# Mixture-of-experts block: the second expert product with its weights standing, each choice's result in a row of its own, and the sum moved into layer 1

## The chip, the cores and the metric

One core of a Trainium2 chip. The metric is the time of one execution on the device, in microseconds; the kernel before takes 15654.79 (median of 3 runs, 15653.87 to 15655.51). All data are fp32.

The engines are named as in the profile: PE multiplies matrices (PEld is its loading of the standing operand), DVE and ACT work on rows and columns of the on-chip memory, POOL does some of the same and issues the indirect transfers (scatters), SP issues the plain transfers. Each works through its own list of instructions in order.

## The reference

Two layers on an image batch x of 32 x 128 channels x 56 x 56. Layer 0 is a depthwise 7x7 convolution, a layer norm over the channels and a mixture of eight experts. T = 100,352 tokens, each with C = 128 values; every token goes to its two best experts, as far as these have room (cap = 15,680 rows for each):

```
xf      = layernorm(dwconv7x7(x))                  # T x C
logits  = xf @ Wg + bg ; top 2, softmax of the two -> wts
order   = argsort(-wts[:, 0])                      # strongest first
slot    = expert * cap + position in the expert    # those beyond cap are dropped
buf[slot] = xf rows ;  eb = buf as E x cap x C
h       = gelu(eb @ W1 + b1) ;  y = h @ W2 + b2    # C -> 4C -> C
moe     = sum over a token's two choices of y[slot] * gate
x       = x + xf (turned back to channels first) + layer_scale * moe
```

Layer 1 is a Mamba block on the result: a 1x1 convolution cv1, a depthwise 3x3 branch, a layer norm and a selective scan over the 3136 positions of each image with 256 channels and 16 states, a last 1x1 convolution, and x added.

## The kernel before

It runs through four stages, and the tensors between them lie in device memory.

Convolution and norm. The convolution is done with banded matrices on two image rows at a time, so a tile of TT = 112 rows of data is two image rows, in an order that is the reverse of the image's (partition p of a tile is position 55 - p of its row). The rows xf go to `res_d` (T x 128) in this reversed order.

Routing (from L478). The choices are ranked, and each token's two slots and gates come out as `slots` and `gates`. Meanwhile SP fills all slots of `buf_d` (L482 to L486) from one tile: zeros and, in column C + 1, the row number T. A row of `buf_d` has RW = 130 columns: the token's 128 values, its gate, and the number of its row in the result.

Dispatch (L840 to L863). 56 turns; each loads 14 x 128 rows of `res_d` into `xgs[0]` (L853), copies them to `xgs[1]` on ACT (L854), adds gate and row number on DVE (L856, L857; the row numbers `backs` are the same for both choices), and issues 28 scatters of 128 rows to `buf_d` on POOL (L859). Six pairs of buffers. Layer 1's weights are prepared in the middle (`weights`).

Experts (L914 to L957). For each expert 31 groups of up to GT x 128 = 512 rows (30 full ones and one of 320). A group is loaded (L945), turned on PE (L951, to `ept`), copied to `xc` on ACT (L953); the products of a group come one group later, in `products`: for each quarter k of the 512 hidden values `ph` = w1 times xc, Gelu on ACT to `hh` (L890, L893); then for each tile of 128 rows `py` += hh (standing) times w2 (moving, 128 columns; L897), so the result comes out with rows on partitions; bias and gate on DVE (L903, L906); and one scatter of 128 rows for each tile on POOL that adds to `res_d` (L911). The adding scatters of one expert are declared independent of each other (`apart`), those of two experts are not.

Layer 1 (`layer1`). 224 groups of 448 positions, 16 states each. The order of all instructions is written out: `PLAN` and `UNITS` give every step a time in units of one state, all steps of all groups are sorted by it and issued in this order. The scan runs on DVE (L1373), its products on DVE and POOL (L1397), the sum over states on PE (L1286), exponentials on ACT (L1354). For each group `fetch` loads the image's columns `x1` and the rows `yg` of `res_d`; `moe_pe` adds them on PE: `x1` times the identity, and each tile of `yg` turned by a product with `perm`, which also undoes the reversed order; `moe_act` copies the sum to `x1`. The matmul tiles `mm_tile` of layer 1 rotate over two banks.

## Time and profile before

| | us |
|---|---|
| median of 3 runs | 15654.79 |
| the profiled execution | 15660.14 |
| its span, first to last instruction | 15658.4 |
| first dispatch scatter (L859) starts | 1772.5 |
| last dispatch scatter starts | 3765.1 |
| first transpose of the experts (L951) | 3770.5 |
| last scatter of the experts (L911) starts | 5688.3 |
| first db product of layer 1 (L1336) | 5738.0 |

Busy time over the whole span: PE 12820.1 us (82%), PEld 7165.1 (46%), DVE 11115.5 (71%), ACT 10499.2 (67%), POOL 13201.9 (84%). The mean granted PE clock is 0.918.

The profile is one execution, seen instruction by instruction. A row of the groups reads: line, engine, operation, what is written from what, how often; busy time in all and mean of one in ns; idle time of the engine just before them and what ended it. The shares over the whole span are a mean over stages that differ, so stages are read one by one. Ends of PE's instructions are modelled and may overlap the next one; starts are the better measure.

### The profile page before, as it was taken

What the parts mean: (1) busy time and instruction counts of PE and PEld (TensorE: products, weight loads), DVE (VectorE), ACT (ScalarE), POOL (GpSimd) and SP (SyncE); (2) the same over time, 40 slices, a digit from 0 to 9 for tenths busy, and PEclk for the clock granted to TensorE, in tenths of its full rate; (3) what the DMA queues carried; (4) which work ended last, traced back from release to release, by engine and by line L of the source; (5) the groups of instructions that cost most, each with busy time, mean ns of one, the idle gap of its engine ahead of it and who ended that gap; (6) DMA issues with size and microseconds to landing.
All of it is one profiled execution on the core that took longest, in us unless ns stands there. A gap on an engine that the chain in (4) does not pass through costs nothing. (4 is left out here: it accounts for less than half of the span.)

```text
span 15658.4 us, 247520 instructions
## 1 busy us (share of the span) xinstructions
PE 12820.1 (82%) x92981; PEld 7165.1 (46%) x92981; DVE 11115.5 (71%) x11366; ACT 10499.2 (67%) x21038; POOL 13201.9 (84%) x6330
## 2 busy tenths in 40 slices
PE   7997200003999989999999999999999999999998
PEld 7996100002777754444444444444444444444444
DVE  2655500000111149999999999999999999999999
ACT  4555300001444458888888888888888888888887
POOL 2443377777888879999999999999999999999999
PEclk9997555556999999999999999999999999999999
DMA  8785522223555545555555555555555555555555
GB/s 266 232 234 165 189 78 78 78 78 68 72 71 72 70 102 184 183 185 184 183 186 184 183 184 185 183 184 186 185 183 184 185 183 183 185 185 184 183 183 169
DMA packets 1325280, 2520.85 MB, mean 161 GB/s; under 512 B 139352, under 2 KB 777136, under 8 KB 1316400
## 3 DMA queue, kind: packets, MB, share of 16 engines
q1 hardware_dynamic: 1127600, 2310.57, 46.9%
q0 software_dynamic: 196480, 194.45, 7.2%
q8 instruction: 732, 11.99, 0.3%
q14 instruction: 468, 3.83, 0.1%
HBM read 2129.06 MB, written 375.43 MB: 160 GB/s over the span
## 5 line engine op out<-in xcount | busy, mean ns | idle before, releaser
L1336 POOL TENSOR_TENSOR db<-du,bb 128x1792 f32<-128x1792 f32 x1792 | 6578.8, 3683 | 0.1
L1354 ACT ACTIVATE da<-dt,aneg 128x449 f32<-128x449 f32 x7168 | 4539.9, 637 | 375.4 <-DVE r L1095 113.0
L1373 DVE TENSOR_TENSOR_SCAN da<-da,db 128x898 f32<-128x898 f32 x2240 | 4522.2, 2019 | 0.6 <-issue 0.5
L1286 PE MATMUL py<-prod,ident 64*64 64x448 f32 x28672 | 3225.1, 547 | 121.7 <-DVE prod L1397 114.0
L1397 POOL TENSOR_TENSOR prod<-hs,cb 128x896 f32<-128x896 f32 x1344 | 2604.2, 1938 | 231.3 <-issue 156.7
L1397 DVE TENSOR_TENSOR prod<-da,cb 128x896 f32<-128x896 f32 x2240 | 2439.5, 1089 | 134.6 <-DMA cb<-bc_d 18.2
L859 POOL DMA_INDIRECT buf_d<-xg,slot x1568 | 1515.8, 967 | 482.0 <-issue 456.7
L911 POOL DMA_INDIRECT res_d<-ys,xb x984 | 1592.1, 1618 | 331.6 <-issue 286.2
L1373 DVE TENSOR_TENSOR_SCAN hs<-da,db 128x898 f32<-128x898 f32 x896 | 1785.6, 2014 | 0.1
L951 PE MATMUL ept<-ident,xb 128*128 128x128 f32 (+1 forms) x984 | 189.0, 274 | 1917.3 <-DMA xb<-buf_d 1917.3
L1286 PEld LDWEIGHTS py<-prod,ident 64*64 64x64 f32 x28672 | 1008.5, 132 | 1559.8 <-issue 1065.4
L1126 PE MATMUL p_xm<-te,wk 128*128 128x448 f32 x3584 | 1395.5, 540 | 0.0
L903 DVE TENSOR_TENSOR ys<-py,b2t 128x512 f32<-128x512 f32 (+2 forms) x256 | 170.9, 670 | 1696.2 <-PE py L897 1673.4
L856 DVE COPY xg<-gate 128x14 f32<-128x14 f32 x112 | 20.3, 185 | 1741.2 <-DMA buf_d<-xg,slot 1741.2
L854 ACT COPY xg<-xg 128x1792 f32<-128x1792 f32 x56 | 94.5, 1688 | 1684.9 <-DMA buf_d<-xg,slot 1674.0
L897 PEld LDWEIGHTS py<-w2t,hh 128*128 128x128 f32 x7872 | 936.2, 191 | 175.6 <-issue 113.3
L951 PEld LDWEIGHTS ept<-ident,xb 128*128 128x128 f32 (+1 forms) x984 | 124.6, 143 | 1921.0 <-issue 1920.1
L897 PE MATMUL py<-w2t,hh 128*128 128x128 f32 x7872 | 985.0, 278 | 0.3
L1126 PEld LDWEIGHTS p_xm<-te,wk 128*128 128x128 f32 x3584 | 671.4, 189 | 665.5 <-issue 567.7
L379 PE MATMUL pc<-xc,toep 112*112 112x112 f32 (+1 forms) x8192 | 936.7, 270 | 38.3 <-ACT toep L368 34.8
L1377 DVE TENSOR_TENSOR_SCAN hs<-da,db 128x449 f32<-128x449 f32 x896 | 925.6, 1075 | 0.5 <-ACT da L1354 0.3
L1258 PE MATMUL p_l<-xh,dwd 64*64 64x224 f32 x16128 | 907.2, 352 | 21.8 <-ACT dt L1240 1.8
(241 smaller groups left out, 20282.2 us busy)
## 6 DMA issues: line engine op xcount, KB each, us to landing
bb<-bc_d SPq DMA_DIRECT2D x1792, 448.0 KB
cb<-bc_d SPq DMA_DIRECT2D x1792, 448.0 KB
toep<-toep_d SPq DMA_DIRECT2D x448, 392.0 KB
buf_d<-zero SPq DMA_DIRECT2D x28, 2275.0 KB
xb<-buf_d SPq DMA_DIRECT2D x240, 260.0 KB
xt<-in_x SPq DMA_DIRECT2D x32, 1568.0 KB
res_d<-xa SPq DMA_DIRECT2D x128, 392.0 KB
xg<-res_d SPq DMA_DIRECT2D x56, 896.0 KB
```

Of the source, the lines that this page charges most:

```text
L379: nc.tensor.matmul(pc[:, c, :, lo:hi], lhsT=tp[c // 2][:, c % 2, 6 - 2 * o : 8 - 2 * o, :], rhs=s4[:, c, :, lo + o - 1 : hi + o - 1], star ...
L859: apart(nc.gpsimd.indirect_dma_start(out=buf_d[:, :], out_offset=bass.IndirectOffsetOnAxis(ap=slots[k][:, o + j : o + j + 1], axis=0), in_ ...
L897: nc.tensor.matmul(py[:n, j, :], lhsT=hh[:, k, j * 128 : j * 128 + n], rhs=w2t[:, k, :], start=k == 0, stop=k == KF - 1,)
L911: apart(nc.gpsimd.indirect_dma_start(out=res_d[:, :], out_offset=bass.IndirectOffsetOnAxis(ap=xb[:n, j, C + 1 : C + 2].bitcast(I32), axis= ...
L1126: nc.tensor.matmul(p[:, :CH1], lhsT=s["wk"][:, k, hs], rhs=d["te"][:, k : k + CH1], start=k == 0, stop=k == DC - 1 and not first,)
L1258: nc.tensor.matmul(d["p_l"][r][k * HD : (k + 1) * HD, : CH1 // 2], lhsT=s["dwd"][rs, t, rs], rhs=d["xh"][rs, dy + k * R : dy + (k + 1) * R ...
L1286: nc.tensor.matmul(ps[r][h * HD : (h + 1) * HD, :CH1], lhsT=lhsT(rs, h), rhs=rhs[rs, h, :], start=start, stop=stop,)
L1336: nc.gpsimd.tensor_tensor(dbp[i // 2].rearrange("p k (h t) -> p k h t", h=2)[:, :, :, 1:], st[g]["du"].unsqueeze(1).to_broadcast(both), un ...
L1354: e = nc.scalar.activation(da[:, h * W1 : (h + 1) * W1], st[g]["dt"][:, h, :], AF.Exp, scale=s["aneg"][:, h, i : i + 1])
L1373: scans.append(nc.vector.tensor_tensor_scan(hs, da, dbs[i], 0.0, ALU.mult, ALU.add))
L1377: scans.append(nc.vector.tensor_tensor_scan(hs2[h][:, hh], da[:, hh], dbs[i][:, hh], 0.0, ALU.mult, ALU.add))
L1397: eng.tensor_tensor(w["prod"], w["hs"][0][:, :, 1:], w["cb"], ALU.mult)
```

## The change

Zero fill: the row numbers of empty slots are now different for every slot of a block (2T + ...), seven blocks of VF over two tiles `zeros`, so that every slot has a row of its own to scatter to.

Dispatch: the row number of choice k of a token is 2 x (its position in image order) + k. The copy to `xgs[1]` is on DVE. Each turn also writes zeros (`none`) to a piece of `y_d`, the new tensor with two rows for each token. And `skip` is called, 64 times in all (twice in each of the first eight turns, then once): it loads half an image by columns (`xs`) and the same half's rows of `res_d` (`xr`), turns and adds both on PE (`perm` times the rows, and the image's columns by the identity), copies on ACT and stores the rows to `sum_d` from ACT's queue.

Experts: four steps, each a group apart: `enter` (load, turn, copy to `xc`, now on DVE), `hidden` (w1, Gelu), `result` (w2 quarter standing, 512 columns of `hh` moving; the result has channels on partitions; the bias is a column, added on DVE to `yt`), `leave` (turned back on PE to `pb`, times gate on DVE, one plain scatter to `y_d` for each tile). On PE the steps of three groups alternate.

Layer 1: `fetch` loads the rows of `sum_d` and both choices' rows of `y_d`, neighbouring positions on one partition; `moe_pe` turns and adds the three with the identity, each into every fourth column.

```diff
+        FILL = 128 * ZT
+        VF = 7
+        sum_d = dram.tile([T, C], F32, name="sum_d")
+        y_d = dram.tile([2 * T + VF * FILL, C], F32, name="y_d")
...
-            zero = rt.tile([128, ZT, RW], F32, name="zero")
-            nc.gpsimd.memset(zero, 0.0)
-            nc.gpsimd.memset(zero[:, :, C + 1].bitcast(I32), T)
-            buf_t = buf_d[: E * CAP].rearrange("(p k) c -> p k c", p=128)
-            for k in range(0, E * CAP // 128, ZT):
-                nc.sync.dma_start(out=buf_t[:, k : k + ZT, :], in_=zero)
+            zeros = [rt.tile([128, ZT, RW], F32, name=f"zero{k}") for k in range(2)]
+            for zero in zeros:
+                nc.gpsimd.memset(zero, 0.0)
+            buf_t = buf_d[: E * CAP].rearrange("(b p k) c -> b p k c", p=128, k=ZT)
+            for v in range(VF):
+                zero = zeros[v % 2]
+                nc.gpsimd.iota(
+                    zero[:, :, C + 1].bitcast(I32), pattern=[[1, ZT]], base=2 * T + v * FILL, channel_multiplier=ZT
+                )
+                for b in range(v, E * CAP // FILL, VF):
+                    nc.sync.dma_start(out=buf_t[b], in_=zero)
...
+            tc.tile_pool(name="skip", bufs=2, reuse_waits="tile") as sk,
+            tc.tile_pool(name="pskip", bufs=3, space=PSUM) as psk,
...
-                nc.gpsimd.iota(bi, pattern=[[TT, QB], [1, TT]], base=0, channel_multiplier=PT)
+                nc.gpsimd.iota(
+                    bi.rearrange("p q (r w) -> p q r w", w=HW), pattern=[[2 * TT, QB], [2 * HW, 2], [-2, HW]],
+                    base=2 * (HW - 1) + k, channel_multiplier=2 * PT,
+                )
...
+            none = dc.tile([128, 2 * T * C // (128 * QB * (TT // XT))], F32, name="none")
+            nc.vector.memset(none, 0.0)
+            y_t = y_d[: 2 * T].rearrange("(b p k) c -> b p (k c)", p=128, b=QB * (TT // XT))
+            HT = TPI // 2
+            parts = [(n, h) for n in range(N) for h in range(2)]
+            def skip(n, h):
+                t0 = (n * TPI + h * HT) * TT
+                xt = sk.tile([C, HT * TT], F32, name="xs")
+                nc.sync.dma_start(out=xt, in_=x_d[n, :, h * HT * TT : (h + 1) * HT * TT])
+                xr = sk.tile([TT, HT, C], F32, name="xr")
+                rows = [v[t0 : t0 + HT * TT, :].rearrange("(k p) c -> p k c", p=TT) for v in (res_d, sum_d)]
+                nc.sync.dma_start(out=xr, in_=rows[0])
+                for j0 in range(0, HT, 4):
+                    w = min(4, HT - j0)
+                    p = psk.tile([TT, 4, C], F32, name="p_sk")
+                    nc.tensor.matmul(p[:, :w], lhsT=perm, rhs=xr[:, j0 : j0 + w], start=True, stop=False)
+                    for j in range(w):
+                        nc.tensor.matmul(
+                            p[:, j, :], lhsT=xt[:, (j0 + j) * TT : (j0 + j + 1) * TT], rhs=ident,
+                            start=False, stop=j == w - 1,
+                        )
+                    nc.scalar.copy(xr[:, j0 : j0 + w], p[:, :w])
+                nc.scalar.dma_start(out=rows[1], in_=xr)
...
-                    nc.scalar.copy(xgs[1][:, :, :C], xgs[0][:, :, :C])
+                    nc.sync.dma_start(out=y_t[q * (TT // XT) + p0 // XT], in_=none)
+                    nc.vector.tensor_copy(xgs[1][:, :, :C], xgs[0][:, :, :C])
...
+                    for _ in range(-(-len(parts) // (TT // XT * (QB - q) - p0 // XT))):
+                        skip(*parts.pop(0))
...
-            tc.tile_pool(name="eph", bufs=3, space=PSUM) as eph,
+            tc.tile_pool(name="eph", bufs=2, space=PSUM) as eph,
             tc.tile_pool(name="epy", bufs=2, space=PSUM) as epy,
+            tc.tile_pool(name="epb", bufs=2, space=PSUM) as epb,
...
+            def enter(w, e, i0):
...
+                d["xc"] = eb.tile([C, GT * 128], F32, name="xc")
+                nc.vector.tensor_copy(d["xc"][:, :rows], pt[:, :rows])
+                return d
+            def hidden(d, k):
...
+                nc.tensor.matmul(
+                    ph[:, :rows], lhsT=w1t[:, k * 128 : (k + 1) * 128], rhs=d["xc"][:, :rows], start=True, stop=True
+                )
+                nc.scalar.activation(d["hh"][:, k, :rows], ph[:, :rows], AF.Gelu, bias=b1t[:, k : k + 1])
+            def result(d, k):
...
+                nc.tensor.matmul(
+                    d["py"][:, :rows], lhsT=w2t[:, k, :], rhs=d["hh"][:, k, :rows], start=k == 0, stop=k == KF - 1
+                )
+                if k == KF - 1:
+                    d["yt"] = eb.tile([C, GT * 128], F32, name="yt")
+                    nc.vector.tensor_scalar(d["yt"][:, :rows], d["py"][:, :rows], b2t, None, ALU.add)
+            def leave(d):
+                tiles, xb = d["tiles"], d["xb"]
+                pb = epb.tile([128, GT, C], F32, name="pb")
+                for j, n in enumerate(tiles):
+                    nc.tensor.transpose(pb[:n, j, :], d["yt"][:, j * 128 : j * 128 + n], ident)
+                ys = eb.tile([128, GT, C], F32, name="ys", bufs=6)
+                for j, m, n in wholes(tiles):
+                    nc.vector.tensor_tensor(
+                        ys[:n, j:m, :], pb[:n, j:m, :], xb[:n, j:m, C : C + 1].to_broadcast([n, m - j, C]), ALU.mult
+                    )
+                for j, n in enumerate(tiles):
+                    apart(nc.gpsimd.indirect_dma_start(
+                        out=y_d[:, :],
+                        out_offset=bass.IndirectOffsetOnAxis(ap=xb[:n, j, C + 1 : C + 2].bitcast(I32), axis=0),
+                        in_=ys[:n, j, :], in_offset=None,
+                    ), "back")
...
+            for at in line + [None] * 3:
+                new = None
+                if at:
+                    if at[1] == 0:
+                        w = load_weights(at[0])
+                    new = enter(w, *at)
+                one, two, three = held
+                for k in range(KF):
+                    if one:
+                        hidden(one, k)
+                    if two:
+                        result(two, k)
+                if three:
+                    leave(three)
+                held = [new, one, two]
...
-            nc.sync.dma_start(out=d["x1"], in_=x_d[n, :, q * CH1 : (q + 1) * CH1])
-            d["yg"] = two.tile([TT, TPC1, C], F32, name="yg")
-            nc.sync.dma_start(
-                out=d["yg"], in_=res_d[t0 : t0 + CH1, :].rearrange("(j p) c -> p j c", p=TT)
-            )
+            d["yg"] = one.tile([TT, 2 * TPC1, C], F32, name="yg")
+            nc.sync.dma_start(
+                out=d["yg"], in_=y_d[2 * t0 : 2 * (t0 + CH1), :].rearrange("(p j) c -> p j c", p=TT)
+            )
+            d["xg"] = one.tile([TT, TPC1, C], F32, name="xg")
+            nc.sync.dma_start(
+                out=d["xg"], in_=sum_d[t0 : t0 + CH1, :].rearrange("(p j) c -> p j c", p=TT)
+            )
...
-            nc.tensor.matmul(p[:, :CH1], lhsT=ident, rhs=d["x1"], start=True, stop=False)
-            for j in range(TPC1):
-                nc.tensor.matmul(
-                    p[:, j * TT : (j + 1) * TT], lhsT=yg[:, j, :], rhs=perm, start=False, stop=j == TPC1 - 1
-                )
+            for j in range(TPC1):
+                parts = xg[:, j, :], yg[:, 2 * j, :], yg[:, 2 * j + 1, :]
+                for k, rows in enumerate(parts):
+                    nc.tensor.matmul(
+                        p[:, j:CH1:TPC1], lhsT=rows, rhs=ident[:TT, :TT], start=k == 0, stop=k == len(parts) - 1
+                    )
```

The tiles `perm` and the wide `mean_w` move out of the constants that stay for the whole kernel; `load_weights` holds the same loads as before with the bias of the second product as a column.

## The prediction

> **What bounds the kernel now.** I read the busy time by stage first, since the kernel is three programs in a row with different limits. Columns: stage, its length, busy time (and instructions) of PE, PE's weight loads, DVE, ACT, POOL, granted clock, DMA share, GB/s.
>
> ```profile
> 2700.00:3500.00 800.00, 0.00 (x0) 0.00 (x0) 11.69 (x88) 38.30 (x23) 608.23 (x630) 0.50 0.26 78
> 4200.00:5000.00 800.00, 799.88 (x4574) 578.52 (x4575) 147.92 (x226) 344.66 (x523) 666.14 (x413) 1.00 0.54 72
> 5738.00:15658.00 9920.00, 9469.33 (x69860) 4437.75 (x69850) 9761.76 (x7609) 8600.29 (x17823) 9511.08 (x3422) 1.00 0.57 183
> ```
>
> The dispatch (1772 to 3766 us) is POOL issuing scatters. The experts (3770 to 5694) have PE busy all the time. Layer 1 has DVE at 98%, POOL at 96%, PE at 95%. Then the costliest groups:
>
> ```profile
> L911 POOL DMA_INDIRECT res_d<-ys,xb x984 | 1592.1, 1618 | 331.6 <-issue 286.2
> L859 POOL DMA_INDIRECT buf_d<-xg,slot x1568 | 1515.8, 967 | 482.0 <-issue 456.7
> L854 ACT COPY xg<-xg 128x1792 f32<-128x1792 f32 x56 | 94.5, 1688 | 1684.9 <-DMA buf_d<-xg,slot 1674.0
> L897 PE MATMUL py<-w2t,hh 128*128 128x128 f32 x7872 | 985.0, 278 | 0.3
> ```
>
> A dispatch scatter costs 0.97 + 0.30 (issue) = 1.27 us, x1568 = 1994 us: the whole stage. An accumulating scatter of the experts costs 1.56 + 0.30 = 1.86 us, four to a group 7.4 us. Is that or PE the pace? The timeline of PE over one group of 512 rows answers (start, length, instruction; lengths overlap, so I subtract starts):
>
> ```profile
> 4301.69 3.60 PE L890 MATMUL ph<-xc,w1t 128*128 128x512 f32 x8
> 4305.12 0.83 PE L897 MATMUL py<-w2t,hh 128*128 128x128 f32 x6
> 4305.79 0.27 PE L951 MATMUL ept<-ident,xb 128*128 128x128 f32 x1
> 4306.06 3.17 PE L897 MATMUL py<-w2t,hh 128*128 128x128 f32 x26
> 4309.07 0.49 PE L951 MATMUL ept<-ident,xb 128*128 128x128 f32 x3
> 4309.40 3.60 PE L890 MATMUL ph<-xc,w1t 128*128 128x512 f32 x8
> ```
>
> One group is 9.40 - 1.69 = 7.71 us with no gap: 8 instructions of 512 columns at 0.43 (3.43), 32 of 128 columns at 0.115 (3.68), four transposes in 0.60, of which the lone one takes 0.27 and the other three 0.11 each. So PE is the pace, POOL at 7.4 is just below it. 240 full groups and 8 of 320 rows are worth 245: 245 x 7.71 = 1889 of the 1900 us to PE's last product.
>
> **The change, part by part.**
>
> *Zero fill (before L486).* The 28 writes of 2275 KB stay, but now seven row fillings alternate over two tiles, so each filling after the second waits for four earlier writes. Before, the writes ran from 1537 to under 1700 us at 426 GB/s and the slots came at 1766, so some 65 us cover them. Four writes are 9.3 MB, 22 us, during which the other tile refills: cost 0. Without overlap seven turns of about 3 us would be 21, still under the cover.
>
> *Dispatch.* POOL keeps the same 1568 scatters in the same order, so only their starvation or slowing counts. Added traffic: 56 zero writes of 1.84 MB to y_d, 64 half images with 2.4 MB each (image, rows, sum), 257 MB in all, 129 GB/s over 1994 us on top of 78; the zero fill shows 426. On SP each row load now queues behind the half images' loads, which wait for PE and ACT's store. A half image is 14 tiles; per four tiles PE has 2 instructions of 512 and 8 of 128 columns, at the 0.50 clock of this stage 2x0.86 + 8x0.23 = 3.56 us, so 12.5 us, two of them 25 us in the first eight turns, against 28 scatters x 1.27 = 35.6 us; later one per turn. Six buffers run ahead: cost 0. ACT does 64 x 4 copies of some 0.6 us, nothing waits for it but its own stores.
>
> The 128x1792 copy moves from ACT to DVE, 56 times. No row shows DVE copying that much. Upper end: twice the 1089 ns of the 128x896 product at L1397, 2.2 us, if POOL stood still throughout: 56 x 2.2 = 122. Lower end, the row of DVE working from SBUF to SBUF under a scatter:
>
> ```profile
> 1827.30 1.46 DVE L750 TENSOR_SCALAR dwd<-ident,dw 128x128 f32<-128x128 f32 x7
> 1827.31 0.97 POOL L859 DMA_INDIRECT buf_d<-xg,slot  x1 [0.30 <-issue]
> 1828.58 1.02 POOL L859 DMA_INDIRECT buf_d<-xg,slot  x1 [0.30 <-issue]
> ```
>
> At most 0.05 us lost per two us of DVE: 56 x 0.05 = 3. These are seven short operations; one long one cannot slip between two scatters, so I go off the lower end and take +25. [...]
>
> *Experts.* POOL: plain scatters priced like L859, 4 x 1.27 = 5.1 us a group, off the pace; if plain is no cheaper than L911, 7.4 still hides. DVE: the 512-column PSUM copy taken from ACT, bias and gate, 3 x 0.67 (mean at L903) = 2.0 us. ACT: four Gelus, 2.7 us. PE sets the pace again: py with w2 stationary is 8 instructions of 512 columns, 8 x 0.43 = 3.44 in place of 3.68; but the result comes out turned and must be turned back: four more transposes. In the built program the order is four back, four in, then ph and py in turn. Sum: 16 x 0.43 + 8 x 0.11 = 7.76; plus one exposed start as at the lone transpose (0.27 - 0.11 = 0.16) 7.92; with two, 8.08. I take 7.92, one run of transposes per group: 245 x 0.21 = +51 (bounds +12, +91).
>
> DVE also waits for each expert's weights (before up to 9.4 us for w2t and 5.6 for b2t, hidden); now xc and yt queue behind it, one group (7.9 us) ahead of their use: at most 7 us x 6 = 42, mostly covered, +5. One more pipeline stage fills and drains: half a group, +4.
>
> The end of the stage gains. Before, POOL was 18 us behind PE:
>
> ```profile
> 5669.90 1.02 PE L1026 MATMUL p_moe<-x,ident 128*128 128x448 f32 x2
> 5688.30 1.43 POOL L911 DMA_INDIRECT res_d<-ys,xb  x1 [0.30 <-issue]
> 5694.27 2.05 PE L1028 MATMUL p_moe<-perm,yg 112*128 112x112 f32 x8 [23.36 <-DMA yg<-res_d]
> ```
>
> Now after the last product: bias 0.7, transposes 0.6, gate 0.7, three scatters 3.8, landing 2.3 (median at L859), a yg load that took 3 and is now double, 4: 12 in place of 24 us, -12.
>
> *Layer 1.* p_moe was 2 instructions of 448 columns and 8 of 112; it becomes 24 of 112 (three sources, two instructions each, four tiles), written to every fourth column.
>
> ```profile
> 10026.46 1.02 PE L1026 MATMUL p_moe<-x,ident 128*128 128x448 f32 x2
> 10027.32 1.04 PE L1028 MATMUL p_moe<-perm,yg 112*128 112x112 f32 x8
> 10028.74 0.98 PE L1286 MATMUL py<-prod,ident 64*64 64x448 f32 x8 [0.38 <-DVE prod L1397]
> ```
>
> Before: 0.86 + 8 x 0.13 = 1.9; after 24 x 0.13 = 3.1: +1.2 us, x224 = 270 us of PE. PE idles 450 us here, and by the waits list DVE waits only some 20 us in all, so DVE, not PE, is the pace. What queues behind: 0.38 us is taken up at once, ACT's read of p_moe came 1.8 us after its end (10030.16), and PE later waits 1.2 us a group for ACT's xd (266.9 us in all). So nearly everything is absorbed; where the copy of z slips 0.7 us, the exponentials follow with little slack. +10; bounds 0 (all absorbed) and +270 (nothing). The order of the plan is unchanged. On SP the image load is replaced by 448 + 224 KB in runs of 4 and 2 KB; single buffers suffice, since the fetch stands nine steps behind the last read.
>
> Sum: 25 + 51 + 5 + 4 - 12 + 10 = +83 on the profiled execution's 15,660.1 (span 15,658.4 and 1.7 around it): 15,743. The median of the runs is 5.3 lower: **15,738**.
>
> **The rivals.**
>
> *A, as above* (chance 0.50): with the bounds of the expert rate and a dispatch between 3 and 60, cut where slower begins: 15,686 to 15,800.
>
> *B, DVE's copy stops the scatters* (0.12): 122 in place of 25, 15,835. For it: scatters leave only 0.30 us between them. Against: the L750 rows.
>
> *C, PE becomes layer 1's bound* (0.10): +270 in place of 10, about 16,000; half of it 15,868. For it: after the change PE is at 98% too. Against: PE's waits are for ACT's later, paced steps.
>
> *D, not slower* (0.28): the experts stream at 512-column speed throughout. Place: the PE group. The pure rate, columns without starts, is 16 x 0.427 + 8 x 0.107 = 7.68 us, -7; with end and fill -15, and the stage's other 11 us of gaps gone, -26; it decides from a group below 7.73 us with dispatch at its lower 3 (245 x 0.02 = 12 - 4 - 3): 15,632. If layer 1's longer runs also remove DVE's 17.5 us of waiting for cb, 15,614. More likely 15,635 to 15,680. For it: PE has no gaps that the records show. Against: four more transposes every group.
>
> That plain scatters are not cheaper costs nothing until a group falls under 7.4 us.
>
> **How the numbers follow.** A measurement of this kernel can tell about 0.2%, 31 us, from no change. A, B and C are slower: 0.72. D splits at 15,624 into no change 0.20 and faster 0.08. Range 15,640 to 15,890: below it lies D's lower half (about 0.1), above it C's upper half (under 0.1). A's own range is 15,686 to 15,800.
>
> **What would show it.** Scatter row of the dispatch still 967 ns and its stage 1994 us, else B. PE starts one group apart: 7.9 us; 7.7 says D. POOL in the experts about half busy, scatters near 1.0 us. From the last expert product to the first p_moe 12 us. Layer 1 from first db to end 9920 us; DVE waits beyond 20 us and a PE near 99% say C. I am wrong if the dispatch starves for row loads, if writes to every fourth column are slower than 0.13 us, or if an expert group is paced by anything but PE.

## The result, and the profile after

| | before | after |
|---|---|---|
| median, us (20 runs each, taken side by side) | 15,659.7 | 15,682.4 |
| ratio, with its 95% interval | | 1.0015 (1.0008 to 1.0022) |
| profiled span, us | 15,658.4 | 15,677.4 |
| first to last dispatch scatter starts | 1992.6 | 2007.3 |
| last dispatch scatter to first expert transpose | 5.4 | 5.3 |
| first expert transpose to first p_moe of the loaded rows | 1923.8 | 1921.0 |
| that p_moe to the first db product | 43.7 | 48.4 |
| first db product to the end | 9920.4 | 9924.0 |

The forecast was 15,738, 83 us slower than before; measured were 23 between the medians and 19 between the two profiled spans. It lies in the range, but by the 0.2% bound it is no change, and it is 4 us below the likeliest case's own range. The rows of the table give +14.7, -0.1, -2.8, +4.7 and +3.6; the stretch before the first scatter gives -1.1. Their sum is the +19.0 between the spans.

Busy time by stage in the kernel after (columns as in the prediction):

```profile
2700.00:3500.00 800.00, 196.87 (x816) 134.45 (x817) 43.72 (x153) 49.62 (x96) 608.90 (x626) 0.59 0.62 198
4200.00:5000.00 800.00, 800.00 (x2500) 404.11 (x2499) 204.15 (x326) 285.30 (x419) 397.66 (x416) 1.00 0.25 72
5753.00:15677.00 9924.00, 9675.25 (x72976) 4743.97 (x72968) 9765.71 (x7609) 8587.06 (x17823) 9513.13 (x3423) 1.00 0.60 188
```

The dispatch moves 198 GB/s where it moved 78, and POOL is as busy as before, so nothing starves. In the experts POOL has fallen from 666 to 398 of 800 us; PE alone is full, with half the instructions. In layer 1 PE has risen from 9469 to 9675 of some 9920 us.

One expert group on PE, after:

```profile
4603.84 0.60 PE L985 MATMUL pb<-ident,yt 128*128 128x128 f32 x4
4604.27 0.60 PE L953 MATMUL ept<-ident,xb 128*128 128x128 f32 x4
4604.71 1.02 PE L964 MATMUL ph<-xc,w1t 128*128 128x512 f32 x2
4605.57 1.02 PE L974 MATMUL py<-hh,w2t 128*128 128x512 f32 x2
...
4611.58 0.60 PE L985 MATMUL pb<-ident,yt 128*128 128x128 f32 x4
```

From one `pb` to the next it is 7.74 us: eight transposes at 0.11, sixteen instructions at 0.43, and no exposed start anywhere, not at the transposes either.

The groups that answer to the scatters of before, from the page:

```profile
L903 POOL DMA_INDIRECT buf_d<-xg,slot x1568 | 1529.1, 975 | 481.6 <-issue 461.4
L992 POOL DMA_INDIRECT y_d<-ys,xb x984 | 941.3, 957 | 978.4 <-DVE ys L988 735.6
```

A plain expert scatter costs 0.957 us where the adding one cost 1.618. POOL now waits for DVE, so the gain is idle time. In the dispatch the mean rose from 967 to 975 ns, although the median fell to 958; the timeline shows which scatters pull the mean up:

```profile
2510.43 0.96 POOL L903 DMA_INDIRECT buf_d<-xg,slot  x1 [0.30 <-issue]
2511.69 1.44 POOL L903 DMA_INDIRECT buf_d<-xg,slot  x1 [0.31 <-issue]
2511.92 1.09 DVE L898 COPY xg<-xg 128x1792 f32<-128x1792 f32 x1
2513.43 0.96 POOL L903 DMA_INDIRECT buf_d<-xg,slot  x1 [0.30 <-issue]
```

This scatter, under way when DVE's copy starts, takes 0.48 us more and ends 0.12 us after the copy. 44 of the 56 copies meet a scatter in this way; the other 12 meet one that starts 0.04 to 0.58 us into the copy, and it ends 0.82 to 0.95 us after the copy. The mean loss is 0.49 us, 27 us for all, which is also 1568 x (975 - 958) ns.

The end of the experts, after:

```profile
5686.63 0.60 PE L985 MATMUL pb<-ident,yt 128*128 128x128 f32 x4
5687.44 0.55 PE L985 MATMUL pb<-ident,yt 128*128 128x128 f32 x3 [0.21 <-DVE yt L979]
5704.96 0.77 PE L1100 MATMUL p_moe<-ident,xg 112*128 112x112 f32 x2 [16.97 <-DMA xg<-sum_d]
```

The last product ended at 5686.6, so 18 us pass, where before it was 24: three groups are turned back within 3.4 us (5684.0, 5686.6 and 5687.4), so eleven scatters stand in a row from 5685.9 to 5698.5, and only then is `yg` loaded.

### The profile page after: what moved, and what is told of

Read it like the earlier page. It is cut to its first block, busy times and chain, and to the rows that moved or that the text cites. A ratio compares the mean times of both kernels' runs of the same rounds, so it can differ in the third digit from the quotient of the medians.

```text
span 15677.4 us, 249094 instructions
## 1 busy us (share of the span) xinstructions
PE 13564.1 (87%) x93517; PEld 7432.3 (47%) x93517; DVE 11316.5 (72%) x11664; ACT 10384.4 (66%) x20990; POOL 12571.1 (80%) x6337
## 5 line engine op out<-in xcount | busy, mean ns | idle before, releaser
L992 POOL DMA_INDIRECT y_d<-ys,xb x984 | 941.3, 957 | 978.4 <-DVE ys L988 735.6
L967 ACT ACTIVATE hh<-ph,b1t 128x512 f32<-128x512 f32 (+1 forms) x992 | 676.4, 682 | 1278.0 <-PE ph L964 1278.0
L881 PE MATMUL p_sk<-xr,perm 112*112 112x512 f32 (+1 forms) x512 | 318.6, 711 | 1209.9 <-DMA xr<-res_d 1209.9
L887 ACT COPY xr<-p_sk 112x512 f32<-112x512 f32 (+1 forms) x256 | 136.2, 532 | 1606.1 <-PE p_sk L883 1606.1
L979 DVE TENSOR_SCALAR yt<-py,b2t 128x512 f32<-128x512 f32 (+1 forms) x248 | 184.6, 744 | 1392.3 <-PE py L974 1392.3
L964 PE MATMUL ph<-xc,w1t 128*128 128x512 f32 (+1 forms) x1984 | 1006.4, 589 | 0.0
L974 PE MATMUL py<-hh,w2t 128*128 128x512 f32 (+1 forms) x1984 | 1002.9, 587 | 0.0
```

Of the source, the lines that this page charges most:

```text
L964: nc.tensor.matmul(ph[:, :rows], lhsT=w1t[:, k * 128 : (k + 1) * 128], rhs=d["xc"][:, :rows], start=True, stop=True)
L974: nc.tensor.matmul(d["py"][:, :rows], lhsT=w2t[:, k, :], rhs=d["hh"][:, k, :rows], start=k == 0, stop=k == KF - 1)
L992: apart(nc.gpsimd.indirect_dma_start(out=y_d[:, :], out_offset=bass.IndirectOffsetOnAxis(ap=xb[:n, j, C + 1 : C + 2].bitcast(I32), axis=0) ...
```

## The experiments

Eighteen runs of twelve kernels were made in six comparisons, each beside the kernel before on the same chip. The chips turned out to be of two kinds. On the first (that of the result, and of `e1_loads_act`, `e2_sum_dve`, `c12_copy_dve_third` and `e3_loads_act_again`) the kernel before takes 15,653 to 15,660 us. On the second (all others) it takes 15,841 to 15,845, and there the dispatch is longer: 2167 us with the code of before, in place of 1993. The first two groups of the experts also take 19 us more there with that code (first to last transpose 1906 us in `c2_copy_dve`, 1887 in the kernel before on the first kind). Ratios are read within a comparison, stages within a kind.

### What an expert group costs

The lone transpose of before again, now with PE's weight loads (PEld) and ACT beside PE, in the timeline:

```profile
4305.32 0.69 ACT L893 ACTIVATE hh<-ph,b1t 128x512 f32<-128x512 f32 x1 [0.17 <-PE ph L890]
4305.68 0.14 PEld L951 LDWEIGHTS ept<-ident,xb 128*128 128x128 f32 x1
4305.79 0.27 PE L951 MATMUL ept<-ident,xb 128*128 128x128 f32 x1
4306.06 0.30 PEld L897 LDWEIGHTS py<-w2t,hh 128*128 128x128 f32 x2 [0.24 <-ACT hh L893]
4306.06 0.38 PE L897 MATMUL py<-w2t,hh 128*128 128x128 f32 x1
```

The weight load after the transpose stands idle and is released by `hh`: ACT's last Gelu ends at 4305.32 + 0.69 = 4306.01, and the fourth w2 product needs it as its standing operand. The list of that line counts these waits:

```profile
L897 PE MATMUL py<-w2t,hh x7872: 272/275/377, 3777.4 to 5669.7; 128*128 128x128 f32 x195, 128*64 128x128 f32 x2
...
  ACT hh L893: 57.0, 239
```

239 times, 0.24 us each, once per group. So the 0.16 us may not be a start of the transpose but this wait. Two kernels take the wait away in different ways.

`t1_behind_ph`, the kernel before with the transposes between w1 and w2 products (`turn` makes the next group's four):

```diff
                 py = epy.tile([128, GT, C], F32, name="py")
+                turn()
                 for j, n in enumerate(tiles):
                     for k in range(KF):
...
```

> The kernel before with the four transposes of a group between its w1 products and its w2 products, so that no transpose stands inside the w2 products; same instructions, same number. Theory W, the 0.16 us around the lone transpose were not its start: the next w2 product's weight load waited for ACT's last Gelu (idle 0.24 us, released by hh, 238 times). Four transposes, 0.44 us, now cover that Gelu: a group is 3.43 + 3.68 + 0.44 = 7.55 us in place of 7.71, 245 x 0.16 = 39 us go, 15,615 to 15,630 us in all. Rival S, the prediction's reading: a run of transposes pays one exposed start of 0.16 us: 7.71 us a group and 15,659. Rival P, POOL's four scatters (4 x 1.86 = 7.44 us) become the pace: 7.55 is not reached, 7.6 to 7.7, POOL's idle time before a scatter is the 0.30 of its issue alone.

`t4_quarters`, the kernel before with the quarters outside in groups of four whole tiles:

```diff
-                for j, n in enumerate(tiles):
-                    for k in range(KF):
+                even = len(tiles) == GT
+                pairs = [(j, k) for j in range(len(tiles)) for k in range(KF)]
+                if even:
+                    pairs.sort(key=lambda p: p[1])
+                for at, (j, k) in enumerate(pairs):
...
+                        start=at == 0 if even else k == 0, stop=at == len(pairs) - 1 if even else k == KF - 1,
```

> The kernel before with the w2 products of a full group in another order: quarter by quarter of the hidden values, all four tiles within a quarter; so the last Gelu is needed 12 products (2.8 us) after the last w1 product, and the four transposes come in one run right behind a short product of 128 columns. Theory W (a wait for the last Gelu): no wait is left, 7.55 us a group, 15,615 to 15,630 us in all. Rival S (a run of transposes pays a start of 0.16 us): 7.71 us, 15,659. Rival S2 (the start is hidden behind a long instruction only): 7.71 us here, but 7.55 with the transposes behind the w1 products.

Measured: `t1_behind_ph` 0.9967 (0.9955 to 0.9980), 15,791.3 against 15,841.3 us; `t4_quarters` 0.9966 (0.9954 to 0.9978), 15,787.6. PE in `t4_quarters`:

```profile
4600.00 3.60 PE L890 MATMUL ph<-xc,w1t 128*128 128x512 f32 x8
4603.44 3.73 PE L901 MATMUL py<-w2t,hh 128*128 128x128 f32 x32
4607.01 0.60 PE L955 MATMUL ept<-ident,xb 128*128 128x128 f32 x4
4607.44 1.02 PE L890 MATMUL ph<-xc,w1t 128*128 128x512 f32 x2
```

A group is 7.44 us, below the 7.55 of theory W. The four transposes take 0.43 although they follow products of 128 columns, so S and S2 are out. And the 32 products take 3.57, not the 3.68 read before: that 0.11 belongs to the same wait, since the product behind it takes 0.38 us where the others take 0.275 (the row at 4306.06 above). The wait cost 0.27 us a group, 0.16 + 0.11. In `t1_behind_ph` a group is 7.45 us. The waits for `hh` shrink from 239 to 4:

```profile
L901 PE MATMUL py<-w2t,hh x7872: 272/275/582, 3949.8 to 5800.5; 128*128 128x128 f32 x195, 128*64 128x128 f32 x2
...
  ACT hh L893: 17.8, 4
```

POOL's scatters (mean 1556 ns here) with their 0.30 of issue make 7.42 us for four: rival P did not decide, but it is next, 0.02 us below.

Both were run again, `t4_quarters` as `t6_quarters_again` and `t1_behind_ph` as `t7_behind_ph_again`.

> The kernel before with the w2 products quarter by quarter, once more, as the candidate that beats both kernels and as the measure of the dispatch on this comparison's chip (its dispatch is that of the kernel before). From its first run: 7.445 us a group, ratio 0.9966; here 0.9955 to 0.998 on any chip. First to last dispatch scatter 1993 us on a chip like that of the prediction, about 2166 on one like the two of the other comparisons.

> The kernel before with a group's transposes behind its w1 products. 7.445 us a group as on the second kind of chip, experts (first to last transpose) 1887 to 1834-1840 us; ratio 0.9966 (0.9955 to 0.998) on either kind, 15,606 us where the kernel before takes 15,660. Rival (the gain came with the slow dispatch of those chips): less than 20 us.

Measured: 0.9966 (0.9953 to 0.9978) and 0.9969 (0.9957 to 0.9981). All four runs fell on chips of the second kind, so what the order gives on the first is not measured; a group of the kernel before takes 7.71 us on both kinds. On the second kind the order alone beats both kernels: first to last transpose is 1846 to 1856 us in the four runs, where it is 1906 with the order of before. Some 50 us of the 64 that 240 x 0.265 would give arrive; part of the rest are two to four single gaps of 1 to 6 us.

### The row copy on DVE

`c1_copy_act`, the changed kernel with the copy on ACT:

```diff
-    nc.vector.tensor_copy(xgs[1][:, :, :C], xgs[0][:, :, :C])
+    nc.scalar.copy(xgs[1][:, :, :C], xgs[0][:, :, :C])
```

> The changed kernel with the copy of the dispatch's second row buffer back on ACT; nothing else differs. In the changed kernel first to last dispatch scatter takes 2007.3 us (before: 1992.6), and its scatters' mean of 975 ns stands 17 ns above their median. Theory 1, DVE's copy holds up POOL: 1568 x 17 ns = 27 us go, the mean falls to the median of 958 ns, first to last scatter 1980 us (1976 to 1986), the whole 15,655 us (15,645 to 15,662). Rival, the new traffic and the half images' loads slow the scatters (206 GB/s in place of 78): 2005 to 2010 us remain, the whole 15,682. Half of each: 1993, 15,668.

`c2_copy_dve`, the kernel before with the opposite edit:

> The kernel before with that one copy on DVE in place of ACT; no new traffic, no half images. Theory 1, DVE's copy holds up POOL by 0.48 us each time: 56 x 0.48 = 27 us on first to last scatter, 1992.6 to 2019 us if a free scatter stays at 967 ns; about 2007 if the 958 ns of the changed kernel come with ACT's idleness. The whole 15,675 to 15,690 us. Rival, the scatters of the changed kernel were slowed by traffic: here 1992 to 1995 us and 15,660.

Measured, on chips of the second kind: `c1_copy_act` 1.0077 (1.0063 to 1.0090), `c2_copy_dve` 1.0001 (0.9992 to 1.0010). Neither number answers by itself. In `c1_copy_act` the long scatters are gone (longest 1155 ns, mean 958), but POOL now waits for ACT:

```profile
L903 POOL DMA_INDIRECT buf_d<-xg,slot x1568: 952/958/1155, 1776.2 to 4067.6; - x196
...
  ACT xg L898: 263.3, 24
```

ACT's copy stands in its queue behind the half images' copies. In `c2_copy_dve` the dispatch takes 2167.6 us, and 2165.5 with the copy on ACT in `t1_behind_ph`: on this kind of chip, from about 2050 us on, one or two scatters in every 14 or so take 1.8 to 1.9 us, with 0.9 us of idle time in places, whichever engine copies. The cause is not known, and no price of the copy shows through it. The same kernel ran twice more.

> The kernel before with the copy on DVE, once more, because on the first chip the stage was set by something else (2166 us with the copy on ACT as well, scatters of 1.8 and 1.9 us in both). Theory 1 on a chip without those: 56 x 0.48 = 27 us more than the run of this comparison with the copy on ACT, 1993 to 2020 us; with them nothing (0 to 5 us). Rival (DVE's copy costs nothing by itself, the changed kernel's 15 us are traffic): no difference on either.

> The kernel before with the copy on DVE. On a chip of the first kind (before: 15,660 us, scatters of 967 ns throughout): theory 1, DVE's copy holds up POOL by 0.48 us each time, 56 x 0.48 = 27 us: 1993 to 2015-2022 us, the whole 15,685; rival, the changed kernel's 15 us are traffic: 1993 and 15,660. On a chip of the second kind: no difference again, 2167 us.

`c10_copy_dve_again` met the second kind once more: 1.0001 (0.9991 to 1.0010). `c12_copy_dve_third` met the first: 1.0015 (1.0005 to 1.0024), and the dispatch

```profile
L859 POOL DMA_INDIRECT buf_d<-xg,slot x1568: 963/967/1888, 1766.6 to 3785.6; - x196
```

takes 2019.0 us in place of 1992.6: +26.4, without any of the new traffic. The median stays at 967 ns, the mean is 984 (x 1568: 27 us). DVE's copy costs 0.47 us on average (0.21 to 0.92), and theory 1 stands. The scatter ends 0.12 us after the copy in 42 of the 56 cases and 0.83 to 0.94 us after it in the other 14, which start later than 0.04 us into the copy. Two more runs ask for it in the changed kernel.

`c7_two_loads`, no copy at all:

```diff
-    nc.vector.tensor_copy(xgs[1][:, :, :C], xgs[0][:, :, :C])
+    nc.sync.dma_start(out=xgs[1][:, :, :C], in_=res_b[q, :, ps, :])
```

> The changed kernel without the copy: the second row buffer is loaded from the result rows by a DMA of its own, as the first is (51 MB more traffic, no engine copies). Theory 1, DVE's copy holds up POOL: the scatters' mean falls from 975 ns to their median of 958 (on a chip without the long scatters), first to last scatter 2007 to 1980 us. Rival, traffic: the mean stays at 975 ns or rises with the 51 MB, 2007 us or more. Theory 3 for the kernel with the copy on ACT, whose dispatch grew to 2291 us with POOL waiting 263 us for that copy: the half images' work on ACT stands ahead of the copy; here ACT has no part in the row buffers, so POOL's waits for ACT are gone and the stage is not above the changed kernel's. If instead the half images' loads on SP hold up the row loads, POOL's waits for the load of the row buffers grow beyond 24 us.

`c13_copy_act_again`, the edit of `c1_copy_act` once more:

> The changed kernel with the row copy on ACT. On a chip of the first kind: theory 1 (DVE's copy was the 27 us, and ACT has time here): scatters' mean 957 to 959 ns, first to last scatter 2007 to 1978-1985 us, the whole 1.0015 less 27/15,660, 0.9993 to 1.0003 of the kernel before. Rival (ACT's copy comes late behind the half images, as on the second kind): POOL waits more than 100 us for ACT. On a chip of the second kind: 2291 us again, 1.0077.

Both met the second kind: 1.0214 (1.0197 to 1.0231) and 1.0074 (1.0061 to 1.0088). In both the scatters are even (mean 957 and 958, longest 1077 ns), so the long ones belong to DVE's copy; the stage is set by other waits there, 405 us for row loads in the one and 238 for ACT's copy in the other. Whether the copy on ACT would pay on the first kind was not measured.

### The half images

`a1_after` is the changed kernel unaltered:

> The changed kernel itself, on the chip of this comparison. The last comparison ran on a chip on which the dispatch of the kernel before takes 2166 us in place of 1993: every 22 us two scatters take 1.9 and 1.8 us there in place of 0.97. If that is a limit on how fast scatters are taken, and not work of POOL, DVE's copies are hidden in it, and the changed kernel's dispatch takes about the same 2166 us: the ratio is then 1.0015 less 15/15,660, 0.9995 to 1.001. If it is POOL's own, the 15 us come on top, 1.0010 to 1.0022. On a chip without those scatters: 2007 us and 1.0008 to 1.0022 again.

Measured, on the second kind: 1.0174 (1.0157 to 1.0191), 16,117.7 against 15,843.3 us. No theory had that. The list of POOL's waits:

```profile
POOL buf_d L903 <- issue: 504.2, 1545, 26.9
POOL buf_d L903 <- DMA xg<-res_d: 381.2, 14, 32.8
```

(what it waited for: us, times, longest). The dispatch takes 2419 us, and 14 times POOL waits for a row load: the starvation that the prediction had ruled out. SP's list, from 1900 to 3760 us, says where the loads were:

```profile
SPq L874 <- remote: 989.3, 20, 81.9
```

SP stands at the half images' first load, waiting for a buffer, and the row loads queue behind it. Further down the chain ACT's copies of the half images come late:

```profile
2842.81 0.58 ACT L887 COPY xr<-p_sk 112x512 f32<-112x512 f32 x1 [28.32 <-remote]
2844.43 1.06 PE L883 MATMUL p_sk<-ident,xs 128*112 128x128 f32 x4
2869.41 0.58 ACT L887 COPY xr<-p_sk 112x512 f32<-112x512 f32 x1 [26.02 <-remote]
2914.21 0.37 ACT L887 COPY xr<-p_sk 112x256 f32<-112x256 f32 x1 [16.21 <-remote]
```

The copy at 2869.41 does not read the sum that ends just ahead of it at 2845.49. That sum is the last of a half image, 256 columns wide, and its copy is the one at 2914.21, 69 us later; PE is up to three sums ahead. Matched in order, the 256 copies come 20 us after their sums on average and up to 80, by a releaser that the profile does not have; the 24 to 28 us in the expectation for `e2_sum_dve` below are not these delays but idle times of ACT. On the first kind (the kernel after) each follows its sum by 0.04 us, and SP waits for room, not for the halves.

`c8_no_halves` (copy on ACT) and `c9_no_halves_dve` (copy on DVE) leave the half images out and write zeros to `sum_d` (`s_t`) in their place:

```diff
-                    for _ in range(-(-len(parts) // (TT // XT * (QB - q) - p0 // XT))):
-                        skip(*parts.pop(0))
+                    nc.sync.dma_start(out=s_t[q * (TT // XT) + p0 // XT], in_=none[:, : T * C // (128 * QB * (TT // XT))])
```

> The changed kernel with the copy on ACT and the half images left out: the sum of image and rows is not made, its tensor is filled with zeros by writes in the same turns (so the result lacks these terms). Theory 3, the half images' work on ACT stood ahead of the copy: POOL's 263 us of waiting for ACT are gone, the dispatch takes what the kernel before takes on this chip (1968 to 1993 us without the long scatters, 2140 to 2170 with them) and its scatters have no excess over their median. Rival: writes and loads alone hold up the row buffers: 2250 us or more remain. It also tells whether the 9 ns by which a free scatter of the changed kernel is shorter (958 in place of 967) come with the half images: then 967 here.

> The changed kernel, copy on DVE as it is, with the half images left out (their tensor filled with zeros in the same turns, so the result lacks these terms). The half images are to be what drove the changed kernel's dispatch to 2419 us on the last chip (POOL waiting 381 us for row loads): without them no wait for row loads above 30 us is left and the stage is that of the kernel before on this chip, plus up to 27 us for DVE's copies where scatters run freely (1968 + 27 = 1995 at the changed kernel's free rate of 958 ns). Rival (the zero writes and sheer traffic do it): waits for row loads of 200 us or more remain on a chip like the last; or, on a chip like the prediction's, 2007 us.

Measured: 1.0008 (0.9998 to 1.0017) and 1.0007 (0.9998 to 1.0017); both dispatches take 2167 us, with no wait for row loads in the lists. So on this kind of chip the half images, not the zero writes, cost 250 us; whether by their loads and stores or by their work on PE and ACT these two runs can't tell. The shorter free scatter is not theirs: 958 ns in `c8_no_halves` too.

How they hold it up was asked of two kernels, `e1_loads_act` (their loads issued from ACT's queue: `nc.sync.dma_start` becomes `nc.scalar.dma_start` for `xs` and `xr`) and `e2_sum_dve` (their copies on DVE: `nc.scalar.copy` becomes `nc.vector.tensor_copy`).

> The changed kernel with the two loads of each half image issued from ACT's queue in place of SP's; SP then has the row loads and the zero writes alone. Theory Q, what stands behind the blocked load on SP: SP waited 954 to 989 us at the load of the image columns for a buffer, and POOL 381 to 388 us, 14 or 15 times, for the row loads queued behind it. With the loads on ACT's queue POOL's waits for row loads fall below 30 us and first to last scatter goes from 2419 to 2165 to 2200 us. The half images may then still be unfinished when the dispatch ends and hold up ACT's first Gelus: if the chain of a half image stays as slow as it is while POOL scatters, up to 250 us come back between the last dispatch scatter and the first scatter of the experts, and the whole stays near 16,110. If they keep up: 15,860 to 15,890. Rival (traffic slows the row loads): POOL's waits stay above 200 us.

> The changed kernel with the half images' copies out of PSUM on DVE in place of ACT (the stores stay on ACT's queue). Theory R, ACT is what comes late (its copies wait 24 to 28 us after PE's sums while POOL scatters, with no releaser in the profile): on DVE the copies follow PE's sums within a microsecond, the chain keeps up, POOL's waits for row loads go and the dispatch falls to 2165 to 2200 us. Rival (any engine that follows PE there is late, the releases themselves come late while POOL scatters): DVE waits as long as ACT did, 2380 to 2450 us remain; and as DVE's row copy then stands behind these copies, POOL also waits for DVE, up to 300 us more as with the row copy on ACT.

> The changed kernel with the half images' loads on ACT's queue. On a chip of the second kind (before: 15,843 us, the changed kernel 16,117 with 381 us of POOL's waiting for row loads): theory Q, POOL's waits for row loads fall below 30 us, first to last scatter from 2419 to 2165-2200 us; what is unfinished of the half images may show up again between the last dispatch scatter and the first product of the experts. Rival, traffic: waits above 200 us remain. On a chip of the first kind: 2007 to 2015 us and 1.0016 again, since nothing waits there.

All three met the first kind, where POOL waits for no row load: 1.0016 (1.0006 to 1.0025), 1.0020 (1.0010 to 1.0030), 1.0015 (1.0005 to 1.0024), dispatches of 2012, 2012 and 2009 us. They show that the queue of the half images' loads and the engine of their copies make no difference there. In `e1_loads_act` ACT's copies come up to 28 us after their sums, and the dispatch does not feel it. For the second kind it stays open whether SP's queue or ACT's lateness is the cause, and why ACT comes late. It does so without half images too: in `c2_copy_dve`, behind the last dispatch scatter (3939.8 us), ACT waits 4.9 and 8.5 us for a releaser that the profile does not have, in the first two expert groups.

### PE's slack in layer 1

`m2_moe_four` adds one product (times zero) to each of the four tiles of layer 1's sum, `m3_one_choice` leaves the second choice out:

```diff
-                parts = xg[:, j, :], yg[:, 2 * j, :], yg[:, 2 * j + 1, :]
+                parts = xg[:, j, :], yg[:, 2 * j, :]        # m3; m2 adds a fourth, xg times zeros
```

> The changed kernel with four more products of 112 columns in layer 1's sum of each group (times zero, so the sum is the same): 8 instructions of 0.112 us, 0.90 us a group, 224 groups, 201 us of PE, where PE idles 249 us of layer 1's 9924. Theory (PE's idle time is filled before anything is late, as the changed kernel's own 0.8 us a group were: +4 us): first db product to the end grows by 20 us or less, PE is 99% busy. Rival (the idle time lies where it can't be used, or a later sum holds up the copy and cv1): half or more of it shows, +100 to +201 us.

> The changed kernel with layer 1's sum of the rows and the first choice alone; the second choice is left out of the result. Eight products, 16 instructions of 0.112 us in place of 24: 0.9 us less a group, 201 us of PE in all. The run with four more products a group cost 176 of the 201 us it added (first to last p_moe 10,000 in place of 9824 us), so PE's usable slack was almost gone in the changed kernel. Theory (a threshold: below it DVE sets the pace): taking the same amount away gives back only what the changed kernel lost against the one before, 5 to 10 us (9815 to 9820 us). Rival (PE is the pace on both sides): 100 us or more are gained.

Both met the second kind: 1.0277 (1.0260 to 1.0294) and 1.0168 (1.0152 to 1.0183) of the kernel before, where the changed kernel itself has 1.0174. From the first to the last of these sums' products it took 9824 us in `a1_after`, 10,000 in `m2_moe_four` and 9809 in `m3_one_choice`. Adding 201 us of PE costs 176, taking 201 away gives back 15. It is a threshold, and the changed kernel sits almost on it. What PE still waits for in `m2_moe_four`:

```profile
PE p_dt L1270 <- ACT xd L1263: 155.5, 186, 0.9
```

nearly what it is in the kernel after (174.6): this idle time lies in a chain within the group, and the added work did not fill it. PE sets the pace at 97.8% busy, since 176 of 201 us added to it show; it does not get to 99%.

## Why the prediction was wrong

*The step that failed: "plus one exposed start as at the lone transpose (0.27 - 0.11 = 0.16) 7.92".* No start was exposed. The 0.16 us was a wait of the next product for ACT's last Gelu, which kept company with the transpose because the order had placed them side by side. The change moves `hh` from the standing to the moving side and uses it a group later, so the wait goes. Priced by what the runs showed: before 3.43 + 3.57 + 0.44 + 0.27 of waiting = 7.71; after 16 x 0.429 + 8 x 0.11 = 7.74. The term is 245 x 0.03 = +7 us in place of +51. From the first transpose to the last product the whole came to +3.2 us. The sum of instructions, 7.76, was right; so was "the order is four back, four in".

Between the two spans the forecast was +83 and the result +19. Of the 64 us between them the experts with their end hold 51 (+48 forecast, -2.8 measured), the dispatch 10, layer 1 and what stands ahead of it 2, and the other two stretches 1.

The mechanism that held is rival D's, streaming without exposed starts, which had 0.28. Its pure rate is the slope of the traces, 0.833 ns a column: (0.429 - 0.109) us between instructions of 512 and of 128 columns. Its condition of a group below 7.73 us was missed by 0.01, and the dispatch's real cost kept the result above its 15,635 to 15,680.

*Dispatch, +25 predicted, +14.7 measured.* The copy on DVE holds up scatters, and "I go off the lower end" was right: +26.4 in `c12_copy_dve_third` by itself, 0.47 us a copy. That it is so near to 25 is luck, since the figure was chosen between 3 and 122 and no row gave it; no run shows the 60 at the upper end of A's dispatch either, only these 26.4. Nor does POOL stand still for the whole copy: 42 of the 56 scatters in `c12_copy_dve_third`, and 44 of 56 in the kernel after, end 0.12 us after the copy. So a scatter under way loses not the copy's 1.1 us, but what lies between its own end and 0.12 us after the copy's. The others, which start later than 0.04 us into the copy, end 0.82 to 0.95 us after it in these two runs.

In the changed kernel 1568 x 9 ns = 14 us are given back by a free scatter of 958 ns, whose cause none of the runs found: it is there without the copy and without the half images, and in `m2_moe_four`, which differs from `a1_after` in layer 1 alone and ran on the same chip, it is 962. Two sums of the prediction are off, without weight: 1568 x 1.27 is 1991 us and not 1994, and the upper bound of A adds up to 15,813. The row of short operations taken as the lower end does not carry over to a long one; the reason given for going above it, that a long operation cannot slip between two scatters, does.

*No starvation, "cost 0".* True on the first kind of chip (SP waits for room, POOL's idle time is its issue). On the second the half images cost 250 us: POOL waits 381 us there for row loads that stand behind theirs on SP, the queue that the prediction names and prices at 0. Nothing in the one profile told of that.

*DVE waits +5, fill +4, end -12.* Waits for weights cost nothing that shows: PE waits 0.2 us in all after its first transpose. The end gave -6, not -12: eleven scatters stood in a row where three were counted, since the last groups come out faster than POOL scatters them. With the +3.2 up to the last product, first transpose to first p_moe comes to -2.8.

*Layer 1, +10 predicted, +3.6 measured, and 4.7 more ahead of it.* The instructions cost 0.112 us, before and after, not 0.13, so p_moe grew by 0.9 us and not 1.2 (PE's busy time 9469 to 9675 us, over 224 groups); the "0.8" in the expectation for `m2_moe_four` is too low. That nearly all is absorbed was right. The 4.7 us ahead of the first db product were not in the sum: PE runs the longer sums there with nothing beside them, at a granted clock of 0.50 and 0.21 us an instruction. The reason given, 450 us of idle PE, was a poor one: `m2_moe_four` shows that the next 0.9 us a group is not absorbed. Rival C was 0.10 by judgement and about one such step away in fact.

*Zero fill 0, plain scatters worth nothing.* Both held (-1.1 us; POOL half busy).

## What to carry to other kernels

A short instruction that shows a long time is not priced by its own row: look at the row behind it, on every queue of the engine, for what released it. Here a 0.27 us wait per group was hidden from the list of PE's waits, showed up on the weight loads alone, and was worth more, removed by another order of the same products, than the whole rewritten expert stage. Idle time of an engine is slack only as far as the chain that leaves it can move: test it by adding work, since 249 us of it were worth 25.

## What the runs showed of the hardware that was not expected

The fp32 copy of 128 x 1792 within SBUF on DVE (1.09 us in the kernel after) delayed the scatter that POOL was issuing by 0.47 us on average (0.21 to 0.92, `c12_copy_dve_third`). A scatter under way ended 0.12 us after the copy (42 of 56); one that started later than 0.04 us into the copy ended 0.83 to 0.94 us after it (14 of 56). With the same copy on ACT (1.69 us in the kernel before) no scatter took longer than 1096 ns there (mean 967) and 1155 ns in `c1_copy_act` (mean 958).

The chips of these runs differed by stage: the code of before took 1993 us for its dispatch on some and 2165 to 2168 on others (`t1_behind_ph`, `t6_quarters_again`, and with the copy on DVE `c2_copy_dve`, `c10_copy_dve_again`), with 19 us more at the start of the experts and layer 1 within 7 us, and a change that cost 0.15% on the first kind cost 1.7% on the second. In the traces of the second kind waits in the dispatch are often put to "remote" or "issue" (989 us of SP's and 257 us of DVE's in `a1_after`), so the releases themselves are missing there; what delays them is open.
